# Equal start addresses modulo 256 bytes for the float32r operands of a three-layer graph network on one core

## The chip, the cores and the metric

The kernel runs on one core of a Trainium2 chip. Its time is the device time of one execution in microseconds (us); less is better. A core has engines that work side by side, each with its own queue: TensorE (PE in the profile; PEld is its loading of weights), VectorE (DVE), ScalarE (ACT), GpSimd (POOL) and SyncE (SP), and 16 DMA engines. The on-chip memory has 128 partitions; the place of a tile is a byte offset that is the same in all partitions.

## The reference

The input has 2500 nodes of 256 features (`x`) and 80,000 edges (`src`, `dst`), sorted by `dst`. The nodes are normalized over their features and cut at zero, pass three edge convolutions, and all four stages together are multiplied by `Wf`; the result is added to `x`.

```python
def _edge_conv(x, src, dst, W, b):
    xi = x[dst]
    xj = x[src]
    m = jnp.concatenate([xi, xj - xi], axis=-1) @ W + b
    s = jax.ops.segment_sum(m, dst, num_segments=N)
    cnt = jax.ops.segment_sum(jnp.ones((dst.shape[0],), m.dtype), dst, num_segments=N)
    return s / jnp.maximum(cnt, 1.0)[:, None]
...
h = jnp.maximum(_layernorm(x, axis=-1), 0.0)
xs = [h]
for W, b in ((W0, b0), (W1, b1), (W2, b2)):
    h = jax.nn.relu(_edge_conv(h, src, dst, W, b))
    xs.append(h)
out = x + jnp.concatenate(xs, axis=-1) @ Wf + bf
```

## The kernel before, in words

The sums over edges are written as products with a matrix of edge counts, `a`: its rows are source nodes, its columns destination nodes, and an element says how many edges join the two. With the upper half of `W` called Wt and the lower Wb, a layer is the mean over the incoming edges of `h @ Wb`, plus `h @ (Wt - Wb)`, plus the bias. There are 20 node tiles of 128 (`NT`), and the destinations stand in five groups of 512 columns (`GS`; the last has 452). Features lie on partitions in `hT`, in two halves (`DC`).

**The first 54 us** load and normalize `x`, sort the edges into windows of six destinations, and make the products of the first layer.

**First layer, up to about 190 us.** For each window VectorE compares keys with a running number (`compare`, into `one_m` and `one_n`), TensorE multiplies the two bf16 matrices of ones (`counts`), and ScalarE copies the counts from the bank into `a` (`take_counts`). In between TensorE runs the products of the group before (`Group.multiply`). A finished `a` is stored to device memory for the later layers by GpSimd's queue. The order of all these steps is written out by hand: the strings `order` and `later` list one- and two-letter acts, and `InOrder` keeps each engine in program order. Most instructions pass through that class, and so most rows of the profile name its line, L267; they are told apart by the names of their tiles.

**Second and third layer, about 190 to 312 us and 312 to 434 us.** First a node stage: for ten pairs of node tiles, `Nodes.multiply` multiplies `hT`, split in three parts (tile `staged`), by the weights, split in three forms (tile `block`), 12 products a pair; `Nodes.parts` splits the result in a high part `zh` and a low part `zl`; `combine` and `sums` make four sums of quarters of it, also in high and low (`sh`, `sl`). `Alone.multiply` adds eight products for the last group of 452 columns. Then the long stage (`Stream.run`): the other four groups in two pairs, each by seven products of blocks instead of eight. `Pair.make` turns the counts, loaded as bf16 into `staged`, into float32r `block`s, and `Pair.multiply` runs, for each of seven units and five chunks, four products: high and low for each of two parts. `Pair.own` adds the terms of the nodes themselves, four of them as float32 products with `wsum`. At the end of a pair's products VectorE and ScalarE combine the seven results into `hT`.

**A last stage of 18 us** multiplies the third layer's nodes by the last part of `Wf` and stores the output.

A product is one TensorE instruction with its loading of weights: the moving operand is a row of up to 512 columns in each partition (`a` or `block`: 2048 bytes of float32r), and the weights are a row of 128 columns (512 bytes) of `zh`, `zl`, `sh`, `sl` or `staged`. Where those rows begin follows from the tile's place and from these two helpers, in which even and odd node parts are the two halves of one tile:

```python
def tile_of(z, t):
    return z[:, t % 2, t // 2 * D:(t // 2 + 1) * D]
...
def sums_of(z, q):
    return z[:, q % 2, q // 2 * 2 * D:(q // 2 + 1) * 2 * D]
```

The tiles of a pool lie behind one another in the order in which the program asks for them, each rounded up to 32 bytes. The pool `const` holds `acc`, `hT`, `zh`, `zl` and then small constants; behind it lie `wpool` (tiles `wt`), `early` (keys and `cnt`), `hot` (`one_m`, `one_n`, `own_w`, `own_h` and others) and the first `a`. In the later layers `tmps`, `stage` and `late` (`sh`, `sl`) take the room behind `wpool`, and `block` lies in a pool at the other end of the memory.

Of the kernel before, what the change touches and what calls it, by code (L numbers as in the profile page):

```python
# [8 lines left out]
F32 = mybir.dt.float32  # L9
# [243 lines left out]
F32R = mybir.dt.float32r  # L253
BF16 = mybir.dt.bfloat16
# [44 lines left out]
def by_windows(ctx: ExitStack, tc: tile.TileContext, x, src, dst, Ws, bs, Wf, bf, out, missing):  # L299
# [3 lines left out]
    P = 128  # L303
    N, D = x.shape
# [5 lines left out]
    DC = D // P  # L310
# [15 lines left out]
    N0 = NT * KEEP  # L326
    N1 = NT * (W - FROM)
    BW = 4
    TURN = 4
    AT_ONCE = 3  # L330
# [6 lines left out]
    Q = NT // 2  # L337
# [12 lines left out]
    const = ctx.enter_context(tc.tile_pool(name="const", bufs=1))  # L350
# [3 lines left out]
    early = first_layer.enter_context(tc.tile_pool(name="early", bufs=1))  # L354
    hot = first_layer.enter_context(tc.tile_pool(name="hot", bufs=2))
# [23 lines left out]
    def bank():  # L379
        return ps[-1].tile([P, 512], F32, name="bank")  # L380


    acc = const.tile([P, NT, D], F32, name="acc")
    hT = const.tile([P, DC, NP], F32, name="hT")

    zh = const.tile([P, 2, Q * D + 32], F32R, name="zh")
    zl = const.tile([P, 2, Q * D + 32], F32R, name="zl")
    key_m = early.tile([P, NW + 1, CH, REP], BF16, name="key_m")
    key_n = early.tile([P, NW + 1, CH, REP], BF16, name="key_n")
    away = early.tile([P, WG, CAP], BF16, name="away")  # L390
    cnt = early.tile([P, NP], BF16, name="cnt")
    share = const.tile([P, NT], F32, name="share")
    per = const.tile([P, NT], F32, name="per")
    brow = const.tile([P, D], F32, name="brow")
# [9 lines left out]
    back_b = const.tile([P, P + 1], BF16, name="back_b")  # L404
    ident_b = back_b[:, 1:P + 1]

    const.tile([P, 16], F32, name="between")
    pairs = [(0, 1), (2, 3)]
    alone = NG - 1
    assert NG == 5  # L410
# [49 lines left out]
    def load_wt(l, queue=SP):  # L460
        queue.dma_start(ws[l][0], Ws[l][0:D, :].rearrange("(c p) d -> p c d", p=P))

    def load_wf(l, queue=SP):
        if l == L:
            new_raw(l)
        wfs[l] = raws[l][:, :, 1, :] if l else hot.tile([P, DC, D], F32, name="own_w1", bufs=1)
        queue.dma_start(wfs[l], Wf[l * D:(l + 1) * D, :].rearrange("(c p) d -> p c d", p=P))
# [24 lines left out]
    def load_b(l, queue=SP):  # L492
        queue.dma_start(brow[PAD:PAD + 1, :], bs[l].rearrange("(o d) -> o d", o=1))
# [222 lines left out]
    def shares():  # L716
        cnt_n = bank()
        for t in range(NT):
            PEo.matmul(cnt_n[:, t:t + 1], cnt[0:1, t * P:(t + 1) * P], ones_b, start=True, stop=True)
        found = hot.tile([P, 1], F32, name="found", bufs=1)  # L720


        fewer = hot.tile([P, NT], F32, name="fewer", bufs=1)
        DVEo.tensor_scalar(fewer, cnt_n[:, :NT], float(256 // 3), None, op0=OP.min)
        DVEo.reduce_sum(found, fewer, axis=mybir.AxisListType.X)
        yield
        pf = bank()
        PEo.matmul(pf[0:1, 0:1], found, ones, start=True, stop=True)
        DVEo.tensor_scalar(missing, pf[0:1, 0:1], float(E), None, op0=OP.not_equal)
        yield  # L730
        some = hot.tile([P, NT], F32, name="some", bufs=1)
        DVEo.tensor_scalar(share, cnt_n[:, :NT], 1.0, None, op0=OP.max)
        DVEo.reciprocal(per, share)
        DVEo.tensor_scalar(some, cnt_n[:, :NT], 1.0, None, op0=OP.min)
        DVEo.tensor_mul(share, per, some)
        yield
# [100 lines left out]
    def compare(b):  # L837
        if b >= len(windows) or b in ones_of:
            return
        g, s, nb = windows[b]  # L840
        w0 = GWS[g][0] + s
        two = b > 0 and b + 1 < len(windows) and windows[b + 1][0] == g
        nb += windows[b + 1][2] if two else 0
        one_m = hot.tile([P, 2 * BW * CH, P], BF16, name="one_m", bufs=AT_ONCE)
        one_n = hot.tile([P, 2 * BW * (N0 + N1)], BF16, name="one_n", bufs=AT_ONCE)
        one_n = one_n[:, :nb * (N0 + N1)].rearrange("p (w n) -> p w n", w=nb)
        for one, iota, keys_ in (
                (one_m[:, :nb * CH, :], iota_m,
                 key_m.rearrange("p w j r -> p (w j) r")[:, CH * w0 + 1:CH * (w0 + nb) + 1, :]),
                (one_n[:, :, :N1], iota_n[:, NB - N1:], key_n[:, w0 + 1:w0 + nb + 1, 0, :]),  # L850
                (one_n[:, :, N1:], iota_n[:, :N0], key_n[:, w0:w0 + nb, 1, :])):
            to = one.rearrange("p k (m r) -> p k m r", r=REP)
            DVEo.tensor_tensor(
                to, iota.rearrange("p (m r) -> p m r", r=REP).unsqueeze(1).to_broadcast(list(to.shape)),
                keys_.unsqueeze(2).to_broadcast(list(to.shape)), op=OP.is_equal)
        ones_of[b] = one_m, one_n, one_m
        if two:
            ones_of[b + 1] = one_m[:, BW * CH:, :], one_n[:, BW:, :], one_m
# [3 lines left out]
    def top_up():  # L862
        if len(ones_of) < len(windows):
            compare(len(ones_of))
# [32 lines left out]
    def by_count(g):  # L897
# [22 lines left out]
        "Z": lambda q: product(q, ws[0][1]), "V": lambda q: with_b(), "H": split_high, "L": split_low,  # L920
        "F": lambda q: product(q, wfs[0]), "G": first_final,
        "B": compare, "C": counts, "E": lambda b: take_counts(b, a),
    }
    order = """
# [13 lines left out]
    late_w, late_forms, late_banks = [], [], {}  # L938
# [33 lines left out]
    def early_loads():  # L972
        assert len(ones_of) == len(windows)
        flat_ = [hot.tile([P, 2 * BW * CH, P], BF16, name="one_m", bufs=AT_ONCE).rearrange("p k m -> p (k m)"),
                 hot.tile([P, 2 * BW * (N0 + N1)], BF16, name="one_n", bufs=AT_ONCE)[:, :2 * DC * D]]
        raws[1] = flat_[0].bitcast(F32).rearrange("p (c t d) -> p c t d", c=DC, t=2)
        ws[1] = flat_[1].bitcast(F32).rearrange("p (c d) -> p c d", c=DC), raws[1][:, :, 0, :]
        SPo.dma_start(ws[1][1], Ws[1][D:2 * D, :].rearrange("(c p) d -> p c d", p=P))
        load_wf(1, SPo)
        load_wt(1, SPo)  # L980
        load_b(1, SPo)
        late_w.append(hot.tile([P, 2 * BW * (N0 + N1)], BF16, name="one_n", bufs=AT_ONCE)[:, :2 * DC * D].bitcast(F32)
                      .rearrange("p (c d) -> p c d", c=DC))
        SPo.dma_start(late_w[0], Wf[0:D, :].rearrange("(c p) d -> p c d", p=P))

# [169 lines left out]
    def take_next(it=iter(range(len([b for b in windows if b[0] == 0]), len(windows)))):  # L1155
# [7 lines left out]
        "y": each((by_count, (g,)) for g in range(NG)), "p": each((split_own, (g, c)) for g in range(1, NG) for c in range(DC)),  # L1163
        "f": each((finish, (g,)) for g in range(NG)), "x": each((add_x, (t, t + 5)) for t in range(0, NT, 5)),
        "s": stepped(shares()), "l": stepped(own_weights()), "k": early_loads, "n": stepped(first_forms()),
        "v": stepped(forms_of_late()), "q": each((late_product, (c, q)) for c in range(DC) for q in LATE),
        "h": each((late_final, (q,)) for q in LATE),
# [28 lines left out]
    tmps = ctx.enter_context(tc.tile_pool(name="tmps", bufs=6))  # L1196
    stage = ctx.enter_context(tc.tile_pool(name="stage", bufs=4))
    late = ctx.enter_context(tc.tile_pool(name="late", bufs=1))
    sh = late.tile([P, 2, Q * D + 32], F32R, name="sh")
    sl = late.tile([P, 2, Q * D + 32], F32R, name="sl")  # L1200
    wsum = late.tile([P, 4, P], F32, name="wsum")


# [383 lines left out]
def gnn_kernel(tc: tile.TileContext, x, src, dst, Ws, bs, Wf, bf, out):  # L1587
    nc = tc.nc
    with tc.tile_pool(name="flag", bufs=1) as flag:
        missing = flag.tile([1, 1], I32, name="missing")  # L1590
        tc.mark_branch_hint_location("again", "LikelyTaken",
                                     engines=[getattr(mybir.EngineType, e) for e in ("PE", "DVE", "Activation")])
        near_end = by_windows(tc, x, src, dst, Ws, bs, Wf, bf, out, missing)
        loads, (again,) = nc.values_load_multi_w_load_instructions(missing, min_val=0, max_val=1)

        for d in loads:
            if d.ins.engine in [getattr(mybir.EngineType, e) for e in ("PE", "DVE", "Activation")]:
                tc.add_manual_dep(d.ins, near_end.ins.name,
                                  mybir.DependencyInfo(mybir.DependencyClass.Sync, mybir.DependencyReason.DATA),
                                  reason="behind the outputs")  # L1600
        with tc.If(again > 0, label="again"):
            general(tc, x, src, dst, Ws, bs, Wf, bf, out)
# [28 lines left out]
```

## Time and profile before

| | |
|---|---|
| Median of 3 runs | 457.06 us (457.0 to 459.65) |
| The profiled execution | 457.22 us, of which 455.3 are the span from the first to the last instruction |
| TensorE, products | 446.1 us busy, 98% of the span, 2755 instructions |
| TensorE, loading of weights | 360.7 us, 79% |
| VectorE | 381.5 us, 84% |
| ScalarE | 327.7 us, 72% |
| GpSimd | 52.4 us, 12% |
| DMA | 54.69 MB, mean 120 GB/s |

A group of instructions is named "out<-in" by its tiles, with shape, type and count, then its busy time and the mean length of one in ns. Products are pipelined: one starts before the one ahead has ended, so in a stream of products the distance from start to start, which the timeline shows, is what each costs; the length of one is larger. The timeline merges neighbours of the same name into one row with a count; its columns are start and length in us, then engine and instruction. The chain that ended last is followed back from the last instruction to what released it.

### The profile page before, as it was taken

The numbers are of one execution on the slowest core, as the hardware profiler recorded it, in microseconds if no ns is written. First come the engines' busy times: TensorE is split into PE (matmuls) and PEld (weight loads), VectorE is DVE, ScalarE is ACT, GpSimd is POOL, SyncE is SP. The second block draws the span as 40 slices with busy tenths as digits, with TensorE's granted clock in tenths as the row PEclk, the third lists the DMA queues.
The fourth block names the chain that finished last, engine by engine and source line by source line (L and its number), as shares of the span: only waits on it lengthen the run. The fifth ranks groups of instructions, "written<-read, shape, count | busy, mean of one in ns | idle before, by whom it ended". The sixth has DMA issues, their size and how long they took to land.

```text
span 455.3 us, 7523 instructions
## 1 busy us (share of the span) xinstructions
PE 446.1 (98%) x2755; PEld 360.7 (79%) x2755; DVE 381.5 (84%) x736; ACT 327.7 (72%) x610; POOL 52.4 (12%) x68
## 2 busy tenths in 40 slices
PE   7999999999999999999999999999999999999995
PEld 3888877888888788888877878877888778788795
DVE  7999989998899635399968958996999688688995
ACT  5898788777765335587879968875877999497730
POOL 4790201302007010100000000000000000000000
PEclk9999999999999999999999999999999999999998
DMA  8410099791969998611392442211124625232015
GB/s 273 118 37 1 15 198 169 87 171 27 201 125 100 179 227 177 143 51 46 125 360 64 140 168 94 92 48 46 47 63 177 247 94 184 94 105 80 1 64 166
DMA packets 28489, 54.69 MB, mean 120 GB/s; under 512 B 1963, under 2 KB 20094, under 8 KB 28446
## 3 DMA queue, kind: packets, MB, share of 16 engines
q0 software_dynamic: 12576, 19.31, 25.7%
q1 hardware_dynamic: 14366, 33.21, 22.1%
q10 hardware_dynamic: 1504, 1.63, 1.0%
q8 instruction: 23, 0.38, 0.3%
q14 instruction: 20, 0.16, 0.1%
HBM read 35.85 MB, written 18.45 MB: 119 GB/s over the span
## 4 chain that ended last, share of the span: by engine, by line
PE 88%; DVE 3%; POOL 3%; DMA 2%; SPq 1%; issue 1%; ACT 1%; ACTq 0%
PE bank L267 88%; DMA one_n<-in_L_gnn_Wf_dram 1%; DVE st L267 1%; POOL acc L267 1%; SPq L267 1%; DMA acc<-in_x_dram 1%; POOL es L267 1%; POOL ed L267 1%; DVE mv L267 0%; ACT one_m L267 0%; DVE acc L267 0%; ACT hT L267 0%; DVE pick L267 0%; DVE one_n L267 0%; DVE wt L267 0%
## 5 line engine op out<-in xcount | busy, mean ns | idle before, releaser
L267 ACT CAST block<-staged 128x1024 fp32r<-128x1024 bf16 x120 | 119.2, 1044 | 3.7 <-ACT block L267 3.2
L267 PE MATMUL bank<-a,zh 128*128 128x512 f32 (+1 forms) x200 | 80.4, 402 | 0.4 <-ACT a L267 0.4
L267 PE MATMUL bank<-block,zh 128*128 128x512 f32 (+1 forms) x200 | 78.4, 392 | 0.0
L267 PE MATMUL bank<-a,zl 128*128 128x512 f32 (+1 forms) x200 | 77.9, 389 | 0.0
L267 PE MATMUL bank<-block,zl 128*128 128x512 f32 (+1 forms) x200 | 76.3, 382 | 0.0
L267 ACT CAST a<-bank 128x480 fp32r<-128x480 f32 (+2 forms) x107 | 53.1, 560 | 27.6 <-PE bank L267 27.5
L267 PE MATMUL bank<-block,sh 128*128 128x512 f32 x160 | 70.0, 437 | 0.0
L267 DVE TENSOR_TENSOR one_m<-iota_m,key_m 128x2048 bf16<-128x2048 bf16 (+3 forms) x55 | 64.3, 1170 | 6.0 <-PE bank L267 5.6
L267 PE MATMUL bank<-block,sl 128*128 128x512 f32 x160 | 63.1, 394 | 0.0
L267 PE MATMUL bank<-block,staged 128*128 128x512 f32 (+1 forms) x288 | 62.1, 368 | 0.0
L267 PEld LDWEIGHTS bank<-block,staged 128*128 128x128 f32 x288 | 49.4, 189 | 9.3 <-issue 0.8
L267 DVE TENSOR_TENSOR block<-staged 128x1024 fp32r<-128x1024 bf16 x40 | 47.3, 1221 | 4.3 <-PE bank L267 3.6
L267 PEld LDWEIGHTS bank<-a,zh 128*128 128x128 f32 x200 | 37.6, 188 | 8.0 <-ACT a L267 0.5
L267 PEld LDWEIGHTS bank<-block,zh 128*128 128x128 f32 x200 | 37.6, 188 | 7.8 <-issue 0.6
L267 PEld LDWEIGHTS bank<-a,zl 128*128 128x128 f32 x200 | 37.7, 188 | 7.5 <-issue 0.5
L267 PEld LDWEIGHTS bank<-block,zl 128*128 128x128 f32 x200 | 37.6, 188 | 7.2 <-issue 0.6
L267 DVE TENSOR_TENSOR one_n<-iota_n,key_n 128x640 bf16<-128x640 bf16 (+3 forms) x110 | 43.0, 432 | 0.0
L267 PEld LDWEIGHTS bank<-block,sh 128*128 128x128 f32 x160 | 30.1, 188 | 11.5 <-issue 3.1
L267 PEld LDWEIGHTS bank<-block,sl 128*128 128x128 f32 x160 | 30.2, 189 | 10.0 <-issue 3.8
L267 PEld LDWEIGHTS <-one_m 128*128 128x128 bf16 x840 | 29.3, 97 | 7.6 <-issue 4.4
L267 PE MATMUL bank<-own_w,hT 128*128 128x256 f32 x144 | 34.6, 384 | 0.0
L267 PE MATMUL bank<-one_n,one_m 128*128 128x60 bf16 x840 | 32.5, 195 | 0.0
(198 smaller groups left out, 667.9 us busy)
## 6 DMA issues: line engine op xcount, KB each, us to landing
staged<-a_dram SPq DMA_DIRECT2D x50, 512.0 KB, 4.7
a_dram<-a POOLq DMA_DIRECT2D x24, 640.0 KB, 11.1
acc<-in_x_dram POOLq DMA_DIRECT2D x3, 640.0 KB, 21.2
out_dram<-acc SPq DMA_DIRECT2D x5, 256.0 KB
acc<-in_x_dram SPq DMA_DIRECT2D x2, 512.0 KB
acc<-in_x_dram ACTq DMA_DIRECT2D x1, 768.0 KB
out_dram<-acc SPq DMA_DIRECT2D x5, 128.0 KB, 2.7
wt<-in_L_gnn_W_dram SPq DMA_DIRECT2D x2, 256.0 KB
```

The source lines that it names most:

```text
L267: return self.tc.keep_in_program_order(call(*args, **kwargs))
```

## The change

Only the places of tiles change; no instruction, transfer or wait is added, removed or moved. An unused tile of 64 bytes, `between`, is asked for ahead of `acc` instead of behind the constants. The 32 unused words at the end of each half of `zh`, `zl`, `sh` and `sl` go. An unused tile of 192 bytes is put behind `cnt`, `found` grows from one word to 16 (of which the first is used), and the three tiles `one_n` grow by 64 bytes.

```diff
+    const.tile([P, 16], F32, name="between")
     acc = const.tile([P, NT, D], F32, name="acc")
     hT = const.tile([P, DC, NP], F32, name="hT")
 
-    zh = const.tile([P, 2, Q * D + 32], F32R, name="zh")
-    zl = const.tile([P, 2, Q * D + 32], F32R, name="zl")
+    zh = const.tile([P, 2, Q * D], F32R, name="zh")
+    zl = const.tile([P, 2, Q * D], F32R, name="zl")
...
     cnt = early.tile([P, NP], BF16, name="cnt")
+    early.tile([P, 48], F32, name="behind_cnt")
...
-    const.tile([P, 16], F32, name="between")
...
-        found = hot.tile([P, 1], F32, name="found", bufs=1)
+        found = hot.tile([P, 16], F32, name="found", bufs=1)[:, 0:1]
...
-        one_n = hot.tile([P, 2 * BW * (N0 + N1)], BF16, name="one_n", bufs=AT_ONCE)
+        one_n = hot.tile([P, 2 * BW * (N0 + N1) + 32], BF16, name="one_n", bufs=AT_ONCE)
...
-    sh = late.tile([P, 2, Q * D + 32], F32R, name="sh")
-    sl = late.tile([P, 2, Q * D + 32], F32R, name="sl")
+    sh = late.tile([P, 2, Q * D], F32R, name="sh")
+    sl = late.tile([P, 2, Q * D], F32R, name="sl")
```

The other two requests for `one_n`, in `early_loads`, grow in the same way.

More of the change, by code (lines that the diff above doesn't have):

```diff
@@ L974, in early_loads @@
         flat_ = [hot.tile([P, 2 * BW * CH, P], BF16, name="one_m", bufs=AT_ONCE).rearrange("p k m -> p (k m)"),
-                 hot.tile([P, 2 * BW * (N0 + N1)], BF16, name="one_n", bufs=AT_ONCE)[:, :2 * DC * D]]
+                 hot.tile([P, 2 * BW * (N0 + N1) + 32], BF16, name="one_n", bufs=AT_ONCE)[:, :2 * DC * D]]
         raws[1] = flat_[0].bitcast(F32).rearrange("p (c t d) -> p c t d", c=DC, t=2)
@@ L981, in early_loads @@
         load_b(1, SPo)
-        late_w.append(hot.tile([P, 2 * BW * (N0 + N1)], BF16, name="one_n", bufs=AT_ONCE)[:, :2 * DC * D].bitcast(F32)
+        late_w.append(hot.tile([P, 2 * BW * (N0 + N1) + 32], BF16, name="one_n", bufs=AT_ONCE)[:, :2 * DC * D].bitcast(F32)
                       .rearrange("p (c d) -> p c d", c=DC))
```

## The prediction

> **What bounds the kernel now.** I read the page's shares first, then the chain that ended last, then the waits of TensorE, and then single products in the timeline, because the change touches nothing but places in memory.
>
> ```profile
> span 455.3 us, 7523 instructions
> PE 446.1 (98%) x2755; PEld 360.7 (79%) x2755; DVE 381.5 (84%) x736; ACT 327.7 (72%) x610; POOL 52.4 (12%) x68
> ...
> PE 88%; DVE 3%; POOL 3%; DMA 2%; SPq 1%; issue 1%; ACT 1%; ACTq 0%
> ```
>
> TensorE is busy 98% of the span and is 88% of the chain. The waits of TensorE alone say that it hardly waits for anyone: its longest entry is the start of the program, and the only later ones are a few tenths.
>
> ```profile
> PE bank L267 <- DVE idle L516: 1.6, 1, 1.6
> PE bank L267 <- POOL acc L267: 0.7, 1, 0.7
> ...
> PE bank L267 <- ACT a L267: 0.4, 1, 0.4
> PE bank L267 <- DVE own_h L267: 0.3, 1, 0.3
> ```
>
> So from 54 us to the end the time is a sum of distances between the starts of products. The stretches show how near the helpers are (columns: length, then busy time and count of PE, PEld, DVE, ACT, POOL, then the granted clock; it is 1.00, so no product is slowed by the clock):
>
> ```profile
> 54.00:157.00 103.00, 102.70 (x998) 81.97 (x998) 94.12 (x174) 72.42 (x199) 22.29 (x23) 1.00 0.87 136
> 157.00:174.00 17.00, 16.72 (x126) 13.76 (x123) 7.27 (x18) 7.24 (x16) 2.22 (x4) 1.00 1.08 222
> 193.00:231.00 38.00, 38.00 (x172) 31.84 (x171) 35.79 (x78) 29.55 (x51) 0.00 (x0) 1.00 0.32 104
> 231.00:310.00 79.00, 79.00 (x328) 61.02 (x326) 65.80 (x90) 64.81 (x80) 0.00 (x0) 1.00 0.37 123
> ```
>
> **How long one product takes, and on what that depends.** The groups of matmuls, kept apart by shape, give the counts of the float32r products (their mean ns is start to modelled end, not the distance between starts):
>
> ```profile
> L267 PE MATMUL bank<-block,sh 128*128 128x512 f32 x160 | 70.0, 437 | 0.0
> L267 PE MATMUL bank<-a,zh 128*128 128x512 f32 x160 | 65.6, 410 | 0.4 <-ACT a L267 0.4
> L267 PE MATMUL bank<-a,zl 128*128 128x512 f32 x160 | 63.2, 395 | 0.0
> L267 PE MATMUL bank<-block,sl 128*128 128x512 f32 x160 | 63.1, 394 | 0.0
> L267 PE MATMUL bank<-block,staged 128*128 128x512 f32 x216 | 53.2, 396 | 0.0
> L267 PE MATMUL bank<-block,zh 128*128 128x512 f32 x120 | 48.4, 403 | 0.0
> L267 PE MATMUL bank<-block,zl 128*128 128x512 f32 x120 | 47.1, 392 | 0.0
> L267 PE MATMUL bank<-block,zh 128*128 128x452 f32 x80 | 30.1, 376 | 0.0
> ...
> L267 PE MATMUL bank<-tmp,staged 128*128 128x512 f32 x36 | 10.2, 391 | 0.0
> ```
>
> Where does each operand begin? Places follow from the sizes of the tiles in the order of their allocation. Modulo 256 bytes they are, in the kernel before: `acc` and `hT` 160; `zh` and `zl` 160 for even node tiles and 32 for odd ones (the row of 2560+32 words per half is 128 bytes off a multiple of 256); `a` 64; `own_w` 32; `own_h` 96; `sh` and `sl` 224 for even parts and 96 for odd ones; `block`, `staged`, `tmp` and `wt` 224. So before, one family has both operands at 224: the products of nodes with weights (`block` with `staged`, and `block` with `block`). The trace holds an undisturbed run of it at 188.74 us, 24 products between the lone group's `a` products and the next stage:
>
> ```profile
> 186.69 0.37 PE L267 MATMUL bank<-a,zh 128*128 128x452 f32 x1
> ...
> 188.74 5.63 PE L267 MATMUL bank<-block 128*128 128x512 f32 x24
> ```
>
> The timeline asked from 190.5 us on shows its last 18, and what starts behind them:
>
> ```profile
> 190.12 4.24 PE L267 MATMUL bank<-block 128*128 128x512 f32 x18
> 194.21 0.54 PE L267 MATMUL bank<-hT,wt 128*128 128x452 f32 x1
> ```
>
> The first six take (190.12-188.74)/6 = 0.230 us from start to start, the other 18 (194.21-190.12)/18 = 0.2272. The stream with mixed places, in the long stage of seven products (33 rows of one product each from 275.76 to 283.22, of which I show the ends and one inside):
>
> ```profile
> 275.76 0.39 PE L267 MATMUL bank<-block,sh 128*128 128x512 f32 x1
> ...
> 277.16 0.40 PE L267 MATMUL bank<-block,sh 128*128 128x512 f32 x1
> 277.40 0.40 PE L267 MATMUL bank<-block,sl 128*128 128x512 f32 x1
> ...
> 283.22 0.40 PE L267 MATMUL bank<-block,sh 128*128 128x512 f32 x1
> ```
>
> 7.46 us over 32 distances is 0.2331. Same shape, same type, same clock, and 2.5% apart: that is what the change can win. Two more rows for the other stages. In the node stage each run of 12 aligned products follows eight of 452 columns with weights at 160 or 32:
>
> ```profile
> 216.10 0.36 PE L267 MATMUL bank<-block,zh 128*128 128x452 f32 x1
> ...
> 217.73 2.93 PE L267 MATMUL bank<-block,staged 128*128 128x512 f32 x12
> 220.50 0.37 PE L267 MATMUL bank<-block,zh 128*128 128x452 f32 x1
> ```
>
> (220.50-217.73)/12 = 0.2308, and (217.73-216.10)/8 = 0.2038 for 452 columns; in the `a` rows above, ten between 186.69 and 188.74, 0.2050. In the first layer, 12 distances between 140.04 and 142.85 give 0.2342:
>
> ```profile
> 140.04 0.40 PE L267 MATMUL bank<-a,zl 128*128 128x512 f32 x1
> ...
> 142.85 0.40 PE L267 MATMUL bank<-a,zl 128*128 128x512 f32 x1
> ```
>
> **The change part by part.** No instruction, DMA or wait is added or removed; the queues of SP and POOL keep their order.
>
> - `between` (64 bytes) goes from the end of the constants to their front: `acc` and `hT` move from 160 to 224.
> - Without the 32 words, each half row of `zh`, `zl`, `sh`, `sl` is 80 x 256 bytes, so even and odd begin alike, at 224; and `zl` lies 20,480 bytes behind `zh`.
> - All later constants move down by 512 bytes net, a multiple of 256. `behind_cnt` (+192), `found` (+32) and three `one_n` (+64 each) then bring `own_w`, `own_h` and `a` to 224: for `a`, 64-512+192+32+192 = -32, which is 224.
> - `block`, `staged` and `tmp` stay at 224. In all the padding takes less memory than the removed gaps gave back.
>
> So every float32r product runs like the run at 188.74, if the places are what made it quick. I take 0.2272 for a stream that nothing disturbs and 0.230 for the first six behind a disturbance. The sum:
>
> 1. Long stage of both later layers: 160+160+120+120+36 = 596 products; I leave 24 out, an allowance for those that stand behind a float32 product or at the start of a stage. 572 x (0.2331-0.2272) = **3.4 us**.
> 2. Node stage: 216 x (0.2308-0.2272) = **0.8 us**.
> 3. 452 columns, 160 with `block` and 80 with `a`: the aligned time isn't in the trace. From 48 aligned products of 256 columns, (440.94-435.18)/48 = 0.120, a column costs (0.2272-0.120)/256 = 0.00042, which makes 0.202 at 452 columns, an estimate from these rows. Against 0.2038 to 0.2050 that is 1.8 to 3.0 ns; 240 times **0.5 us**. The ends are 0 (no effect) and 1.2 us.
>
> ```profile
> 435.18 5.92 PE L267 MATMUL bank<-block,staged 128*128 128x256 f32 x48
> 440.94 1.24 PE L267 MATMUL bank<-wbf,hT 128*128 128x256 f32 x5
> ```
>
> 4. First layer: 320 products with `a`. Groups of counts break the stream about every 12 products (the run above is one such stretch), so some 28 start behind counts, and of the rest half is at 0.230: 292 x (0.2342-0.2286) = 1.6 us. DVE is busy 94.12 of 103 us here and feeds the counts, and between 157 and 174 the chain goes through a load:
>
> ```profile
> 161.93 6.13 DMA one_n<-in_L_gnn_Wf_dram
> ```
>
>    TensorE's gain in that stretch only lengthens its wait for `own_h`. I take half, **0.8 us**; the ends are 0 and 1.9 (all at 0.2272, 0.0065 each, but for those in the load's stretch).
> 5. Counts (840 bf16 products at some 0.03 us) and float32 products get other places too, with no aligned row to compare: 0, with 0.8 us either way (1 ns for each count).
>
> Sum 3.4+0.8+0.5+0.8 = 5.5 us. The profiled execution took 457.22 us (span 455.3 and 1.9 around it), 0.2 over the median of 457.06. 457.22-5.5 = **451.7 us**. Behind TensorE, DVE is next: in the node stage it has 38.00-35.79 = 2.2 us of room, against a gain there of some 0.6, so it does not take over; if its order needs that room elsewhere, up to 0.6 a layer is lost. The output's tail stays.
>
> The rows say that distances differ by 2.5% at equal shape and clock. The Trainium skill (TensorE: Matmul & The Clock Gate, Part 2, step by step) says that TensorE has two independent read ports into SBUF, so that loading the next weights takes no bandwidth from the running product; by its back-to-back formula a 512-column product takes 216 ns wherever it begins. No row here is that quick. By that rule the sum would be 0.
>
> **The rivals.**
>
> *Places don't matter (457.2).* The two streams differ in more than places: the quick run changes its moving block at every product, the slow one uses each block twice. If that, or the semaphore that ends each unit, makes the 6 ns, nothing moves: 457.2 +-0.6. For it: products at equal places in the mixed stream still run from 0.23 to 0.24. Against it: the same kind of run, at equal shape, is 0.2308 behind misplaced products and 0.2272 once undisturbed. The rule above gives this rival.
>
> *Half the effect (454.6 to 456.5).* Equal places help only where both the product's and the next weights' low bits agree beyond 256 bytes, or the quick state is lost at every fresh block. Then 1 to 2.5 us of the 5.5 come.
>
> *The streams lock in the slow state (461 to 465).* Equal places everywhere mean that each weight load, which runs beside the product before it, meets the moving rows always in the same relation. The product at 277.16 has its moving row, its own weights and the next ones at 224, and took 277.40-277.16 = 0.24. If the long stage settles there: 572 x 0.0069 = 3.9 us, the node stage 216 x 0.0092 = 2.0, the first layer 292 x 0.0058 = 1.7, together 7.6 us, 464.8; half as often, 461. It becomes a loss beyond 1% once the mean over some 1,080 products rises by 4.6/1,080 = 4 ns, to 0.237. Against it: in the only long aligned run the stream left 0.23 downwards, not upwards.
>
> **How the numbers follow.** Forecast 0.55, half the effect 0.15, no effect 0.18, slow lock 0.09; 0.03 for a gain beyond the ends. With the upper ends of the terms (3.4+0.8+1.2+1.9+0.8 = 8.1) the time is 449.1; 459 at the top takes in the first three cases and half of a weak slow lock. Left out: the rest of the slow lock and the far gain. A measurement of this kernel tells about 1% from nothing (before: 457.0 to 459.65). Faster by over 1% means below 452.5: most of the forecast's case (451.7, with some 2 us about it) and the far gain, 0.46. Slower: 0.09. The rest, 0.45, is within 1%.
>
> **What would show it.** Right: in the long stage the same 32 distances take 7.3 us, and the run of 12 falls from 2.77 to 2.73; `block,zh` and `block,zl` get the same mean (403 and 392 now); counts of instructions are unchanged. Wrong: distances that still alternate by 5 to 10 ns within a unit (first two rivals), or a stream that sits at 0.236 or above (third); in the first layer a quicker product with the same stretch, if DVE or the load hold it.

## The result and the profile after

The changed kernel takes 455.12 us in the median of 12 executions (453.54 to 458.19); the kernel before took 458.09 in 12 beside it (457.0 to 460.16). The ratio is 0.9935, with an interval from 0.9908 to 0.9962: about 3 us less, where 5.5 were forecast. The profiled execution after took 453.93 us against 457.22, at the same mean granted clock (0.997). The page of the kernel after begins:

```profile
span 452.1 us, 7523 instructions
...
PE 442.8 (98%) x2755; PEld 360.7 (80%) x2755; DVE 381.0 (84%) x736; ACT 327.7 (72%) x610; POOL 51.6 (11%) x68
...
PE 91%; DMA 2%; POOL 2%; DVE 2%; SPq 1%; ACT 1%; issue 1%; ACTq 0%; POOLq 0%
```

Counts of instructions are the same; TensorE still is the chain. Its busy time fell by 3.3 us, as the span did (3.2). The groups of matmuls of the kernel after, kept apart by shape:

```profile
L267 PE MATMUL bank<-block,sh 128*128 128x512 f32 x160 | 69.1, 432 | 0.0
L267 PE MATMUL bank<-a,zh 128*128 128x512 f32 x160 | 64.9, 405 | 0.4 <-ACT a L267 0.4
...
L267 PE MATMUL bank<-block,staged 128*128 128x512 f32 x216 | 53.1, 395 | 0.0
L267 PE MATMUL bank<-block,zh 128*128 128x512 f32 x120 | 47.4, 395 | 0.0
L267 PE MATMUL bank<-block,zl 128*128 128x512 f32 x120 | 46.7, 389 | 0.0
...
L267 PE MATMUL bank<-block,zh 128*128 128x452 f32 x80 | 30.2, 378 | 0.0
```

The groups of 512 columns whose operands came into line are shorter by 3 to 8 ns each (`block,sh` 437 to 432, `block,zh` 403 to 395, `block,zl` 392 to 389). `block,staged`, already at equal places, is where it was (396 to 395), and `block,zh` of 452 columns is 2 ns longer (376 to 378). The timeline of the same stretch of the long stage after, 33 rows that begin two products earlier in the sequence than those of before; the ends and two inside:

```profile
274.20 0.39 PE L267 MATMUL bank<-block,zh 128*128 128x512 f32 x1
...
277.38 0.39 PE L267 MATMUL bank<-block,sh 128*128 128x512 f32 x1
277.61 0.39 PE L267 MATMUL bank<-block,sl 128*128 128x512 f32 x1
...
281.46 0.39 PE L267 MATMUL bank<-block,sh 128*128 128x512 f32 x1
```

7.26 us over 32 distances are 0.2269, where it was 0.2331; no product inside takes 0.24 any more. The first layer and the node stage in the same view, kernel after:

```profile
139.40 0.40 PE L267 MATMUL bank<-a,zl 128*128 128x512 f32 x1
...
142.13 0.39 PE L267 MATMUL bank<-a,zl 128*128 128x512 f32 x1
...
215.56 0.36 PE L267 MATMUL bank<-block,zh 128*128 128x452 f32 x1
...
217.20 2.93 PE L267 MATMUL bank<-block,staged 128*128 128x512 f32 x12
219.97 0.36 PE L267 MATMUL bank<-block,zh 128*128 128x452 f32 x1
```

In the first layer 12 distances take 2.73 us, 0.2275 each (0.2342 before). In the node stage nothing is won: the run of 12 takes 2.77 us as before, and the eight of 452 columns (217.20-215.56)/8 = 0.205, where it was 0.2038.

Stage by stage, the products being the same in the same order, the time from the start of one numbered product to that of another (us):

| stage (number of the product) | before | after | difference |
|---|---|---|---|
| first layer (200 to 1400) | 122.89 | 121.50 | -1.39 |
| last group and its load (to 1521) | 17.26 | 17.55 | +0.29 |
| to the node stage (to 1600) | 14.64 | 14.75 | +0.11 |
| node stage, layer 2 (to 1807) | 46.41 | 46.51 | +0.10 |
| long stage, layer 2 (to 2121) | 76.59 | 75.21 | -1.38 |
| node stage, layer 3 (to 2300) | 40.34 | 40.36 | +0.02 |
| long stage, layer 3 and output (to 2754) | 97.71 | 96.33 | -1.38 |

The sum is -3.63; the 200th product began 0.4 us later (34.2, then 34.6), which gives the 3.2 of the span. That start isn't the change's: another execution of the same kernel had it at 35.6. The two rows of each kernel that bound the long stage of layer 2, before and then after:

```profile
235.38 0.74 PE L267 MATMUL bank<-block,zh 128*128 128x512 f32 x1
...
311.97 1.32 PE L267 MATMUL bank<-block,staged 128*128 128x512 f32 x5
```

```profile
234.91 0.74 PE L267 MATMUL bank<-block,zh 128*128 128x512 f32 x1
...
310.12 3.11 PE L267 MATMUL bank<-block,staged 128*128 128x512 f32 x13
```

76.59 and 75.21 us. In the kernels below, wherever a stage and what stands ahead of it have the places of the changed kernel, the first layer (121.44 to 121.51) and the long stage of layer 2 (75.21 to 75.23) repeat within 0.1 us; the stretch with the load varies more (17.45 to 17.84). So the experiments can be read by these lengths where the time of an execution, which scatters over several us, can't tell.

### The profile page after: what moved, and what is told of

Read it like the earlier page. It is cut to its first block, busy times and chain, and to the rows that moved or that the text cites. A ratio compares the mean times of both kernels' runs of the same rounds, so it can differ in the third digit from the quotient of the medians.

```text
span 452.1 us, 7523 instructions
## 1 busy us (share of the span) xinstructions
PE 442.8 (98%) x2755; PEld 360.7 (80%) x2755; DVE 381.0 (84%) x736; ACT 327.7 (72%) x610; POOL 51.6 (11%) x68
## 4 chain that ended last, share of the span: by engine, by line
PE 91%; DMA 2%; POOL 2%; DVE 2%; SPq 1%; ACT 1%; issue 1%; ACTq 0%; POOLq 0%
PE bank L267 91%; DMA one_n<-in_L_gnn_Wf_dram 1%; POOL acc L267 1%; SPq L267 1%; DMA dst_i<-in_dst_dram 1%; ACT one_m L267 0%; POOL es L267 0%; POOL ed L267 0%; ACT hT L267 0%; DVE pick L267 0%; DVE one_n L267 0%; DVE acc L267 0%; DVE st L267 0%; DVE one_m L267 0%; DVE own_h L267 0%
## 5 line engine op out<-in xcount | busy, mean ns | idle before, releaser
L267 PE MATMUL bank<-own_w,hT 128*128 128x256 f32 x144 | 34.6, 384 | 0.0
```

Source lines behind the costliest of these rows:

```text
L267: return self.tc.keep_in_program_order(call(*args, **kwargs))
```

## The experiments

The main theory (M): the distance of a stream of float32r products follows from how the start of the moving row and that of the weights' row stand to each other modulo 256 bytes. The first rival (W): it is enough that all rows of weights begin alike, whatever the moving row does. A further theory (E) is on what is left in the node stage: the rows of 452 columns (1808 bytes) end 16 bytes past a multiple of 256, and a moving row would have to end where the next one's row begins. All edits are shown against the changed kernel.

### Weights moved away, all by the same

Padding ahead of `zh` and `sh`, so that all their rows begin alike but 64 bytes from the moving rows:

```diff
+    const.tile([P, 16], F32, name="ahead_of_z")
     zh = const.tile(...)
     zl = const.tile(...)
+    const.tile([P, 48], F32, name="behind_z")
...
+    late.tile([P, 16], F32, name="ahead_of_s")
     sh = late.tile(...)
     sl = late.tile(...)
+    late.tile([P, 48], F32, name="behind_s")
```

> All weights' rows that are node parts (zh, zl, sh, sl) begin 64 bytes further on, alike among themselves but no longer alike with the moving rows: 32 against 224 modulo 256. The changed kernel's long stage runs at 0.227 us from start to start. Theory M (the weights must begin where the moving row begins, modulo 256): the long stage goes back to 0.231 to 0.235, the a products of the first layer to 0.232 to 0.234, and the time rises by 3 to 4 us over the changed kernel's 453.9 of its profiled execution. Theory W (the weights must only be alike among themselves): 0.227 and 453.5 to 455.

With 32 words ahead and 32 behind, 128 bytes:

> The same with 128 bytes: weights at 96, moving rows at 224. Theory M: 0.231 to 0.235 as with 64 bytes, possibly another value, since the distance is the largest there is modulo 256. Theory W: 0.227. A rule modulo 128 would give 0.227 here and 0.232 or more with 64 bytes.

With 8 ahead and 56 behind, 32 bytes, to ask whether nearness is enough:

> Weights of the node parts 32 bytes behind the moving rows (0 against 224 modulo 256), the smallest step of places. Theory M in its strict form: no rhythm of 0.227, the long stage at 0.230 to 0.234 as with 64 and 128. If nearness is enough, 0.227 to 0.229.

One unit of 16 products with `sh` and `sl` in the timeline of the long stage, from its first start to the next unit's; first with 64 bytes:

```profile
276.15 0.39 PE L267 MATMUL bank<-block,sh 128*128 128x512 f32 x1
...
279.88 0.39 PE L267 MATMUL bank<-block,zh 128*128 128x512 f32 x1
```

with 128:

```profile
278.08 0.39 PE L267 MATMUL bank<-block,sh 128*128 128x512 f32 x1
...
281.79 0.40 PE L267 MATMUL bank<-block,zh 128*128 128x512 f32 x1
```

and with 32:

```profile
276.25 0.40 PE L267 MATMUL bank<-block,sh 128*128 128x512 f32 x1
...
279.99 0.40 PE L267 MATMUL bank<-block,zh 128*128 128x512 f32 x1
```

3.73, 3.71 and 3.74 us, 0.233, 0.232 and 0.234 for each product: the gain is gone in all three. The times of one execution were 457.77, 459.64 and 457.65, and the long stage of layer 2 took 76.84, 76.64 and 76.73 us, no better than before (76.59). The highest time, 459.64, holds one longer node stage as well (47.50 us, where the other two have 46.49 and 46.28). W falls: the rows of weights are alike among themselves here, with the same halves without gap as in the changed kernel. Nor is the modulus 128 or smaller, and 32 bytes are not near enough. Each misplacement has a rhythm of its own, by the starts in the trace in ns: with 32 bytes distances of 235 and 232 take turns, with 128 a cycle of seven has one of 241, and with 64 they stay at 233 and 234, as in the unit above, or take turns at 231 and 236 in other stretches.

### The moving rows moved away instead

The weights stay at 224; 64 bytes in the pool at the other end move `block` to 160, away from `staged` too:

```diff
     bf_sb.append(raw_pools[-1].tile([P, D], F32, name="bf_sb"))
+    raw_pools[-1].tile([P, 16], F32, name="lower")
```

> Only the blocks, the moving rows of the later layers, begin 64 bytes earlier (160 against weights at 224), which is the same relation as with the weights 64 bytes further on. Theory M: the same 0.233 to 0.234 in the long stage, alternating 0.231 and 0.236; the first layer stays at 0.228; time 2.5 to 3.5 us above the changed kernel.

The unit in its long stage:

```profile
276.94 0.39 PE L267 MATMUL bank<-block,sh 128*128 128x512 f32 x1
...
280.67 0.39 PE L267 MATMUL bank<-block,zh 128*128 128x512 f32 x1
```

3.73 us, with the steady 233 and 234 ns that the unit had with 64 bytes on the other side; the long stage took 76.83 us, the execution 459.69. The runs of 12 with `staged`, at equal places in all other kernels, are now apart as well and take 0.2332 for each product (0.2306 in the changed kernel, means over 14 runs). The `a` products, whose places did not change, stayed at 228 ns and the first layer at 121.51. It is the relation of the two rows, from whichever side it is broken.

### The gaps back, but of 256 bytes

To ask whether the rows must agree beyond 256 bytes (the prediction's second rival), and whether the pitch of the halves matters:

```diff
+    const.tile([P, 64], F32, name="between_z")
     zl = const.tile([P, 2, Q * D], F32R, name="zl")
...
-    sh = late.tile([P, 2, Q * D], F32R, name="sh")
-    sl = late.tile([P, 2, Q * D], F32R, name="sl")
+    sh = late.tile([P, 2, Q * D + 64], F32R, name="sh")
+    sl = late.tile([P, 2, Q * D + 64], F32R, name="sl")
```

> zl begins 256 bytes later against zh, and the halves of sh and sl are set apart by a gap of 256 bytes: everything stays alike modulo 256 and becomes unlike modulo 512. If 256 is the modulus that counts, the long stage stays at 0.227 and the time at 453.5 to 455. If the rows must agree modulo 512 or more (the change made zh and zl alike modulo 4096 as well), the long stage goes to 0.230 to 0.234.

```profile
275.62 0.39 PE L267 MATMUL bank<-block,sh 128*128 128x512 f32 x1
...
279.25 0.39 PE L267 MATMUL bank<-block,zh 128*128 128x512 f32 x1
```

The unit takes 3.63 us, 0.2269 each, and the stages have the lengths of the changed kernel (121.50 and 75.21 us); 454.93 us. Modulo 256 is enough.

### All rows alike, but at another place

Everything moved to 32 modulo 256 (`between` of 128 bytes, and 192 in the other pool):

```diff
-    const.tile([P, 16], F32, name="between")
+    const.tile([P, 32], F32, name="between")
...
+    raw_pools[-1].tile([P, 48], F32, name="lower")
```

> All moving and weights' rows of the float32r products begin at 32 modulo 256 instead of 224. If only the relation between the two rows counts (theory M), the long stage stays at 0.2275 and the a products at 0.228, time 453.5 to 455. If the place 224 itself is special, 0.231 or more.

```profile
275.14 0.39 PE L267 MATMUL bank<-block,sh 128*128 128x512 f32 x1
...
278.77 0.39 PE L267 MATMUL bank<-block,zh 128*128 128x512 f32 x1
```

3.63 us again, stages of 121.50 and 75.23 us, 454.45 us against 456.98 for the kernel before on that chip. Nothing is special about 224.

### The parts of the change alone, timed

Four kernels beside each other on one chip, with 25 executions of the kernel before (median 458.6). The changed kernel once more:

> The changed kernel itself, for comparison on one chip with the others of this call: 0.9935 times the kernel before, as measured, some 3 us less.

454.66 us, ratio 0.9912 (0.988 to 0.9944). Without `behind_cnt`, the larger `found` and the larger `one_n`, so that `a` is back at 64:

> The padding in front of the first layer's tiles is taken back (behind_cnt, found, one_n): a is at 64, own_w at 32 and own_h at 96 again, all else as changed. Theory M: the first layer's 512-column a products go from 0.228 back to 0.233, which is 1.4 us over some 290 of them; the long stage stays at 0.2275; time 1.0 to 1.6 us above the changed kernel, or less if the load at the end of the first layer hides a part.

456.15 us, ratio 0.994 (0.992 to 0.9961). Rows of its first layer:

```profile
140.20 0.39 PE L267 MATMUL bank<-a,zl 128*128 128x512 f32 x1
...
142.77 0.39 PE L267 MATMUL bank<-a,zh 128*128 128x512 f32 x1
```

11 distances in 2.57 us, 0.2336, as before the change; its first layer took 123.02 us, and the rest was as in the changed kernel. By the medians this part is worth 1.5 us, with intervals that overlap, by the stage 1.5 (123.02-121.50); the stretch with the load behind it, 17.08 us where the changed kernel had 17.55, hides a part of that.

The gap of 32 words back in `sh` and `sl` alone:

> Only the gap between the halves of sh and sl is put back, so that odd parts of the sums begin at 96. If every product's own distance follows from its own two rows, only the products beside odd sums slow down: half of sh and sl, a mean of about 0.229 to 0.230 over the long stage, 1.0 to 1.4 us. If the quick rhythm is a state that one unlike row ends and that takes about ten products to come back, nearly the whole long stage goes to 0.231 to 0.233, 2.0 to 2.8 us.

456.52 us, ratio 0.9962 (0.9937 to 0.9987). One unit with `sh` and `sl`, and the unit behind it with `zh` and `zl`:

```profile
275.66 0.39 PE L267 MATMUL bank<-block,sh 128*128 128x512 f32 x1
...
279.38 0.39 PE L267 MATMUL bank<-block,zh 128*128 128x512 f32 x1
...
282.10 0.39 PE L267 MATMUL bank<-block,sh 128*128 128x512 f32 x1
```

The misplaced unit takes 0.2325 for a product (3.72 over 16), the next is back at 0.2267 (2.72 over 12) at once. So the quick rhythm is not lost for good by unlike rows. But it doesn't belong to each pair of rows either. Half of the misplaced unit, the even parts, has its own two rows at equal places; by the starts in ns these products take 227, 232, 235 and 229, and the odd ones 241, 240, 230 and 226. That is 230.8 against 234.3 in the mean: an unlike row slows its neighbours too. The long stages and what follows them are 1.3 us longer than in the changed kernel (0.65 and, in layer 3, 0.68), within the 1.0 to 1.4 that were expected. The medians say 1.9, with intervals that overlap.

### What holds the node stage

Theory E: the rows of 452 columns moved to the end of the block's 512, so that they end where an aligned row ends. They then begin at 208 modulo 256, 16 bytes from the weights:

```diff
-            ACTo.copy(to[:, :, :GS], loaded[p // 2][:, q % 2 * 2:q % 2 * 2 + 2, :])
+            ACTo.copy(to[:, :, GS - self.n:], loaded[p // 2][:, q % 2 * 2:q % 2 * 2 + 2, :self.n])
...
-... tile_of(z, t)[:, o * P:(o + 1) * P], block[:, i, :self.n],
+... tile_of(z, t)[:, o * P:(o + 1) * P], block[:, i, GS - self.n:],
```

> The lone group's 452 columns lie at the end of their row of 512 instead of at its beginning, so the moving row ends at 224 modulo 256, where the next one's row would begin, and begins 240 bytes further on (208). In the changed kernel these products take 0.206 and the runs of 12 behind them 2.77 us. Theory E (a moving row must end where the next begins): 452 columns fall to 0.202, the runs of 12 to 2.73, together 1.0 to 1.5 us off the time. Theory L (a row that is no multiple of 256 bytes breaks the rhythm wherever it lies): 0.203 to 0.207 and 2.77, time unchanged within 0.4 us.

```profile
212.31 2.89 PE L267 MATMUL bank<-block,staged 128*128 128x512 f32 x12
215.04 0.37 PE L267 MATMUL bank<-block,zh 128*128 128x452 f32 x1
...
216.69 2.89 PE L267 MATMUL bank<-block,staged 128*128 128x512 f32 x12
```

The run of 12 now takes 2.73 us, 0.2275 each, the forecast's number. The eight products of 452 columns take (216.69-215.04)/8 = 0.206; over twelve such groups, by the starts in ns, it is 0.2054 where the changed kernel has 0.2057, and far from 0.202. So E's forecast is half right: what these rows leave behind is cured, their own pace isn't. Both the end and the start of the rows moved, so that the end is the reason is not shown. The node stages fell to 46.22 and 40.13 us (46.51 and 40.36). The execution took 453.19 us. Timed beside the others:

> The lone group's columns at the end of their row, timed: the runs of 12 took 2.74 instead of 2.77 us in the one look and the 452-column products 0.205 instead of 0.206, which is 0.43 and 0.15 us over both layers: 0.5 to 0.7 us below the changed kernel, 0.992 of the kernel before.

453.93 us, ratio 0.9913 (0.9883 to 0.9944), against 0.9912 for the changed kernel. The stages say 0.5 us; the times can't tell it from nothing. It is the best version by the profile only.

If the length is what matters, 448 columns (7 x 256 bytes) should do. This kernel leaves out the sums over edges of the last four nodes in the two later layers:

```diff
-PEo.matmul(self.to[o], ..., block[:, i, :self.n], ...)
+PEo.matmul(self.to[o][:, :448], ..., block[:, i, :448], ...)
```

> The lone group's moving rows are cut to 448 columns, a multiple of 256 bytes; the sums over edges of the last four nodes are left out in the two later layers. If it is the row's length that ends the rhythm, these products fall from 0.206 to 0.200 (448 columns at the aligned pace of 0.00042 a column) and the runs of 12 behind them from 2.77 to 2.73 us, as far as no other disturbance lies between. If it isn't, they fall to 0.204 (four columns less) and the runs stay at 2.77.

```profile
213.75 2.91 PE L267 MATMUL bank<-block,staged 128*128 128x512 f32 x12
216.49 0.36 PE L267 MATMUL bank<-block,zh 128*128 128x448 f32 x1
...
218.12 2.91 PE L267 MATMUL bank<-block,staged 128*128 128x512 f32 x12
```

The run of 12 takes 0.2283 for each by these rows (0.2288 in most of the runs), between the two. The eight take (218.12-216.49)/8 = 0.204 by the rows, which are rounded; by the starts in ns it is 0.2027 in the mean of twelve groups. Four columns less would make 0.2057-4 x 0.00042 = 0.2040, and the pace of the prediction's term 3 gives 0.2272-64 x 0.00042 = 0.2003. So a length of a multiple of 256 bytes brings a part of the quick pace, here and in the runs of 12, and not all: neither of the two outcomes that were expected. The execution took 454.45 us (457.49 before on that chip). And the kernel with 32 bytes between the rows speaks against a simple rule on ends:

```profile
213.81 2.89 PE L267 MATMUL bank<-block,staged 128*128 128x512 f32 x12
216.54 0.37 PE L267 MATMUL bank<-block,zh 128*128 128x452 f32 x1
```

Its run of 12 also takes 2.73 us, behind rows of 452 columns that lie as in the changed kernel; only their weights begin 32 bytes further on. What a run finds depends on what stood before it; by which rule stays open, and so does why rows of 448 and 452 columns don't settle.

## Why the prediction was right in kind and too large

**The mechanism, right.** Equal places modulo 256 bytes make the quicker products: shown by taking the agreement away from either side, by 32, 64 and 128 bytes, and by keeping it at another place and with gaps of 256. Why equal places are quicker is not shown, nor whether a product's own weights count or those of the next one, loaded beside it. The rival that places don't matter is out. With it, for this kernel, goes the speed that the prediction drew from the two read ports of the Trainium skill (TensorE: Matmul & The Clock Gate, Part 2, step by step): the same product took 0.2269 or 0.2331 us by places alone. No stream settled at 0.236 or above, so the slow lock is out too. The time came out at the value of "half the effect", but through neither of its causes: 256 bytes suffice, and a fresh block does not lose the rhythm.

**The step that failed** is "every float32r product runs like the run at 188.74". Equal places are enough for that in a stream of 512 columns that runs undisturbed, and not in the node stage: the runs of 12 stayed at 0.2306 and the 452 columns went from 0.2042 to 0.2057 (steps 2 and 3, 1.3 us forecast and a loss of some 0.2 measured). Nor does it hold for the first products behind a float32 one, for which step 1 allowed too little. The steps one by one:

**Step 1, long stage: 3.4 forecast, 2.8 measured** (1.38 in each layer). The full 0.2269 came. The allowance of 24 products for breaks was too small. Rows of the kernel before, and then after, around two float32 products with `wsum`:

```profile
267.63 1.02 PE L267 MATMUL bank<-tmp,wsum 128*128 128x512 f32 x2
...
269.41 1.02 PE L267 MATMUL bank<-tmp,wsum 128*128 128x512 f32 x2
```

```profile
268.35 1.02 PE L267 MATMUL bank<-tmp,wsum 128*128 128x512 f32 x2
...
270.13 1.02 PE L267 MATMUL bank<-tmp,wsum 128*128 128x512 f32 x2
```

1.78 us both times: the four products between two such pairs win nothing. Behind a break the aligned stream needs up to some ten products, of 224 to 236 ns, before it stays at 226 and 227. In the two layers 18 stretches stand behind float32 products, and ten of them are only four products long. The first four of each, 72 products, won nothing (0.1 us lost, by the starts in ns), where the allowance left out 24. At 5.9 ns the 48 more are 0.3 us; the 0.1 lost and later products make up the rest of the missing 0.6.

**Step 2, node stage runs: 0.8 forecast, under 0.1 measured.** The step took the pace of the 24 undisturbed products for runs of 12 that each follow eight of 452 columns. The run stayed at 0.2308. The prediction had seen that a run behind misplaced products is slow, and put it down to their weights alone; with these weights aligned the run is as slow as before, and moving the 452 columns to the row's end cures it (0.2275).

**Step 3, 452 columns: 0.5 gain forecast, a loss measured,** outside the ends that were given (0 to 1.2). In the mean of 12 groups of eight 0.2042 became 0.2057. By the starts in ns the 160 products with `block` lost 0.2 us and the 80 with `a` 0.1, together 0.3. The column price from 256 and 512 columns does not hold for the 448 and 452 columns here. The node stages in all lost just 0.1, so other products there gave some of it back.

**Step 4, first layer: 0.8 forecast, 1.4 measured, 1.1 behind the load.** The half taken off for VectorE was not needed: the stretch to product 1400 kept its 1.4 us, near the whole term (1.6). (The upper end of this step counts 0.0065 for a product; 0.2342-0.2272 is 0.0070, which makes 2.0 us, not 1.9.) What the prediction said of the load holds. Chain in order of time, kernel before (the row of the load stands in the prediction), then after:

```profile
173.06 0.64 DVE own_h L267
173.75 2.26 PE bank L267 x14
```

```profile
160.86 6.51 DMA one_n<-in_L_gnn_Wf_dram
...
172.38 0.64 DVE own_h L267
173.07 3.10 PE bank L267 x18
```

The load starts 1.07 us earlier (161.93 to 160.86), takes 0.38 longer, and the product behind `own_h` starts 0.68 earlier: a part of the gain turned into wait.

**Step 5, other products: 0,** and nothing of size is left over: 2.8 + 1.1 less 0.1 for the node stages and 0.1 ahead of them are the 3.6 of the table, to its rounding. With -0.6, -0.8, -0.8 and +0.3 the four steps take the 5.5 to 3.6. The timed ratios, 0.9935 and 0.9912, are 3.0 and 4.0 us. So the time is within 1% of before, where the prediction gave a little more weight to a larger gain.

**A reading and a sign that don't hold.** The third rival is priced by the product at 277.16, read as one at equal places. By the order in `Pair.multiply` it multiplies an odd part, whose row began at 96 in the kernel before, so its 0.24 says nothing of equal places. And the prediction took an equal mean of `block,zh` and `block,zl` for a sign of being right; they are 395 and 389. Two of the 120 products with `zh` stand right behind float32 products and are 742 ns long; the median of both groups is 389.

## What to carry to other kernels

Where TensorE bounds with float32r products back to back, let the moving row and the weights' row begin alike modulo 256 bytes: here that is worth 6 ns of 233 for each 512-column product, for padding alone. Price it by distances from start to start and behind a float32 product count only those from the tenth on. Float32 products, rows of 452 columns and groups of counts in between take gain away, so that here 596 products of the long stages won as much as some 470 at the full 5.9 ns. A price read from one long undisturbed run isn't the price of a run of 12.

## What the runs showed of the hardware that was not expected

- Aligned, the distance is a steady 226, 227, 227 ns. 32, 64 and 128 bytes apart give 235/232, 233/234 or 231/236, and a cycle of seven up to 241, all with a mean of 232 to 234: among these three it hardly matters how far the rows are apart.
- The quick rhythm is a state that a stream settles into: behind a float32 product it takes up to ten products. Behind a group of counts in the first layer it takes about four (231.5, 230.0 and 228.7 for the second to the fourth in the mean, then about 227.5), and behind a misplaced unit it was there at once (0.2267).
- Rows of 448 and 452 columns at equal places did not reach the pace that 256 and 512 columns suggest (0.2027 and 0.2057 against 0.2003 and 0.202), nor did 452 columns at the row's end (0.2054).
- A run of 12 at equal places took 2.77 or 2.73 us by what stood ahead of it.
